# Layer 1 of a four-layer state-space network: 64x64 sums, and four of sixteen state inputs made by TensorE; in layer 3 the norm at another place

## The chip, the cores and the metric

One core of a Trainium2 chip runs the whole network in one program. The metric is the device time of one execution in microseconds. The core's engines work side by side, each through its own in-order queue: TensorE (PE, matmuls), VectorE (DVE), ScalarE (ACT), GpSimd (POOL), and SyncE (SP), which issues most DMAs.

## The reference

The input is 8 images of 64 channels and 64x64 pixels, float32. Four layers follow each other; layers 1 and 3 matter here. Both hold a selective scan with 128 (layer 1) or 256 (layer 3) channels and 16 states. Cut to the scan of layer 1:

```python
dts, Bs, Cs = jnp.split(x_dbl, [DT_RANK, DT_RANK + N], axis=2)
delta = jax.nn.softplus(dts + dt_b[None, :, :, None])
...
def step(h, inp):
    u, d, b, c = inp
    dA = jnp.exp(d[..., None] * A)
    h = dA * h + d[..., None] * b[:, :, None, :] * u[..., None]
    y = jnp.sum(h * c[:, :, None, :], axis=-1)
    return (h, y)
```

Layer 1 does it in four directions: the pixels by rows, by columns, and both backwards; the four outputs are added, then come a norm over channels, a gate, a projection, a second norm and a feed-forward block with a 3x3 convolution. Layer 3 first scales each pixel by the root of the mean square over its channels (the "norm" of the title), and scans forwards and backwards along one image axis, then along the other.

## The kernel before, in words

`stream` (L462) runs the scans of layers 1, 2 and 3. A **step** is one block of 1024 columns with all 16 **states** n; the loop at L596 runs over states, i counts them through all steps. In layer 1 a step is image b, direction k (in the order `ways` = 1, 3, 2, 0; the odd ones go by columns) and quarter j: 8 x 4 x 4 = 128 steps. In layer 3 it is pass s, chunk c (half an image), group g and direction k: 2 x 16 x 4 x 2 = 256 steps, 8 to a chunk.

For each state of layer 1:

- SP loads row n of B and of C from HBM, broadcast to 128 partitions (`load`, L1339), B five states ahead, C three. B has 4 buffers, C 5.
- GpSimd makes du*B (`multiply_b`, L526), two states ahead, into one of 3 `hb` buffers.
- ScalarE makes dA = exp(dt*A) (`decay`, L520) into one of two PSUM tiles, so it waits for what read the tile two states before. After each scan it copies the last column to `carry` (L1350).
- VectorE scans (L550). It works on one state after the other, and the C product (L564) follows: by VectorE into `hc`, or, for the states in `shared` (1, 4, 7, 10, 13), by GpSimd in place on `h`, one state later.
- TensorE adds the product to `acc` in PSUM (`gather`, `add_up`, L310): a matmul with the identity, 128x128, for each half of the 1024 columns. It is issued two states after the scan. After state 15 `drain` (L1367, L1365) adds `acc` to the image y.

`prepare` (L1317) makes dt, du, B and C for the next step; in layer 1 it starts at state 2 (`start`) and takes a piece per state. The rest of layer 1 (the norms, the convolutions, the feed-forward block: `begin`, `finish`, `feed`) is written as tasks, cut by `yield` into pieces; `advance` (L437) puts a piece into the queues per state. A piece that yields True holds the one "mm" tile of PSUM (`pp`), and nothing else may start that needs it. [...]

Layer 3 uses the same loop with a written plan (`plan`, L2095) of where pieces of `prepare` go. Six states (`fed`: 1, 2, 5, 6, 9, 10) are `direct`: du*B doesn't come from GpSimd. du is turned by TensorE (L2196) into `duT`, B is put on the diagonal of 128x128 blocks in HBM (`place`, L2122) and loaded from there, and `expand` (L2202) multiplies both: 8 matmuls. For the states in `lent` (1, 5, 9) the result goes into a dA tile, and dA of these states goes to SBUF; for 2, 6, 10 it goes into the mm tile. The sums of layer 3 use 64x64 blocks (`quads`, L315), four matmuls that work in the four quarters of the array.

The norm of layer 3 is a task, `begin` (L2034), one per chunk: 8 loads of x; twice a Square (L2053), a mean by TensorE (L2056) and a copy (L2058); Sqrt (L2063), reciprocal (L2066), a trip through HBM to broadcast it, and four products on GpSimd (L2083). It is queued in `behind` by `done` (L2230), after the first step of the chunk before. Pieces that take the mm tile may run at states 7 and 11 only (`rooms`), at 7 only if no `finish` is in `urgent`; a held tile is given back at state 13 (`lets`), or at once where an expansion needs it (L538). While `urgent` holds a task, `behind` stands still.

Of the kernel before, what the change touches and what calls it, by code (L numbers as in the profile page):

```python
# [272 lines left out]
class Net:  # L273
# [163 lines left out]
    def advance(self, behind, room=True, calm=True):  # L437


        while True:  # L440
            queue = self.held or (self.urgent if self.urgent else behind)
            if not queue or not (room or queue[0].said is False):
                return
            task = queue[0]
            if task.calm and not calm:
                return
            task.step()
            self.held = queue if task.said is True else None
            if not task.over:
                return  # L450
            queue.popleft()
# [10 lines left out]
    def stream(self, pools, ahead, steps, behind, rest=None):  # L462
# [39 lines left out]
        def fetch(i):  # L502
            if i < total and not isinstance(bp, tuple):
                s = steps[i // NS]
                t = bp.tile(s.bc_shape, F32, name="bc")
                s.load(i % NS, t)
                B[i], CC[i] = t[:, 0, :] if direct(i) else s.spread(t, 0), s.spread(t, 1)
            elif i < total:
                B[i] = bp[0].tile([128, T], F32, name="b")
                steps[i // NS].load(i % NS, 0, B[i])  # L510
# [22 lines left out]

        def expand(i):
            if i < total and direct(i) and lent(i):
                hb[i] = steps[i // NS].expand(B.pop(i), pe.tile([128, T], F32, name="dA"))
            elif i < total and direct(i):
                while self.held:  # L538
                    self.release()
                hb[i] = steps[i // NS].expand(B.pop(i))  # L540
# [35 lines left out]
            steps[at].add_up(acc[at], hc.pop(i), n == 0 and not begun[at], n == NS - 1)  # L576

        begun = {}
        work, self.held, self.urgent = None, None, deque()
        Task(steps[0].prepare()).run()  # L580
        for i in range(ahead[0]):
# [14 lines left out]
        for i in range(total + 2):  # L596
# [20 lines left out]
            if plan:  # L617
                before, behind_scan = plan.get(n, (0, 0))
                for _ in range(before if work else 0):
                    work.step()  # L620
                work = None if work and work.over else work
                if 2 < i <= total + 2 and shared(i - 3):
                    gather(i - 3)
                if 1 < i and not first and not shared(i - 2):
                    gather(i - 2)
                self.advance(behind, n in steps[0].rooms and not (n == 7 and self.urgent))
                if n in steps[0].lets and self.held:
                    self.release()
                if i < total:
                    scan(i)  # L630
                work = begin_next()
                for _ in range(behind_scan if work else 0):
                    work.step()
                if first:
                    gather(i - 2)
                if i < total and not shared(i):
                    multiply_c(i)
                if not direct(i + 2):
                    decay(i + 2)
                elif lent(i + 2):  # L640
                    expand(i + 2)
                if direct(i + 3):
                    decay(i + 3)
                    if not lent(i + 3):
                        expand(i + 3)
                continue
# [16 lines left out]
            if i < total:  # L663
                if not shared(i):
                    multiply_c(i)
            decay(i + 2)
        steps[-1].drain(acc.pop(len(steps) - 1))
        steps[-1].done()
        while self.held:
# [289 lines left out]
    def layer1(self, src, dst):  # L959
        nc, tc, d = self.nc, self.tc, self.d  # L960
        mid = self.hbm["x1a"]
        with ExitStack() as ctx:
            pool = lambda n, b, **k: ctx.enter_context(tc.tile_pool(name="l1" + n, bufs=b, **k))
            cp, p1, p2, img, tp = pool("c", 1), pool("p1", 1), pool("p2", 2), pool("img", 2), pool("t", 5)
            pp = pool("pp", 1, space=PSUM)
            bp = pool("b", 4), pool("cc", 5)
            pools = (bp, pool("hb", 3), pool("hc", 3), pool("h", 3), two(pool), pool("pa", 1, space=PSUM))

            pp, tp = Choice(pp, pools[4], "dA"), Choice(tp, pools[3], "h")
# [169 lines left out]
            def finish(b, chunks=range(4)):  # L1139
# [5 lines left out]

                def centred(c):
                    ps = pp.tile([128, T], F32, name="mm")
                    self.mm(ps, cent1, y[:, c * T : c * T + T])
                    yield True
                    return ps  # L1150

# [2 lines left out]
                def output(c):  # L1154
# [6 lines left out]
                    yield  # L1161
                    nc.gpsimd.tensor_tensor(inv, inv, z, ALU.mult)
                    ps = pp.tile([128, T], F32, name="mm")
                    self.mm(ps, cent1, y[:, at])
                    yield True
                    yield True
                    nc.vector.tensor_tensor(inv, ps, inv, ALU.mult)
# [21 lines left out]
            def feed(b, part=None):  # L1189
# [80 lines left out]
                for c in range(4):  # L1270
                    if c < 3:
                        yield from normed(c + 1)
                    yield from gated(c)

            def view(t, k, c):

                if k % 2 == 0:
                    return t[:, c * T : c * T + T].rearrange("p (a b) -> p a b", b=HW)
                return t.rearrange("p (a b) -> p b a", b=HW)[:, c * 16 : c * 16 + 16, :]
# [18 lines left out]
                            break  # L1298


            ways = (1, 3, 2, 0)

            class Step:
                start, early, late = 2, 8, True
                plan, direct, add_up = None, (), staticmethod(self.plain_sum)
                shared = (1, 4, 7, 10, 13)
                shaped = staticmethod(lambda t: t)

                def __init__(self, b, k, j):
# [7 lines left out]
                def prepare(self):  # L1317
                    k = self.k
                    u = self.u = view(images[self.b]["u"], k, self.c)
                    pd = pp.tile([128, T], F32, name="mm")[:68]  # L1320
                    net.mm(pd, xp[:, k, :], u)
                    yield True
                    dbl = p1.tile([68, T], F32, name="dbl")
                    nc.scalar.copy(dbl, pd)
                    self.bc = hp.tile([2 * NS, T], F32, name="bc")
                    nc.scalar.dma_start(self.bc, dbl[4 : 4 + 2 * NS])
                    pt = pp.tile([128, T], F32, name="mm")
                    for r in range(2):
                        at, o = slice(r * C, r * C + 4), slice(r * 512, r * 512 + 512)
                        nc.tensor.matmul(pt[:, o], dtw[at, k, :], dbl[at, o], start=True, stop=True)  # L1330
                    yield True
                    yield CALM
                    dt = self.dt = p2.tile([128, T], F32, name="dt")
                    net.softplus_act(dt, pt, dtb[:, k : k + 1])
                    yield False
                    du = self.du = p2.tile([128, T], F32, name="du")
                    nc.gpsimd.tensor_tensor(like(du, u), like(dt, u), u, ALU.mult)

                def load(self, n, m, t):  # L1339
                    nc.sync.dma_start(t, self.bc[m * NS + n : m * NS + n + 1, :].to_broadcast([128, T]))  # L1340
# [6 lines left out]
                def keep(self, n, h):  # L1347
# [3 lines left out]
                    if n == NS - 1:  # L1351
                        images[self.b]["carry"] = self.carry

                def skip(self, acc):
                    if self.k == 0:
                        net.mm(acc, skip[:, 0, :], self.u, start=True, stop=False)
                    return self.k == 0

                def drain(self, acc):
                    hold = images[self.b]  # L1360
                    if self.k == ways[0] and self.j == 0:
                        hold["y"] = img.tile([128, L], F32, name="img")
                    y = view(hold["y"], self.k, self.c)
                    if self.k == ways[0]:
                        nc.scalar.copy(y, like(acc, y))  # L1365
                    else:
                        nc.vector.tensor_tensor(y, like(acc, y), y, ALU.add)  # L1367

                def done(self):
                    b = self.b  # L1370
# [14 lines left out]
            with tc.manual_schedule():  # L1385
# [7 lines left out]
                    begun[1] = Task(begin(1))  # L1393
                    behind.append(begun[1])
                steps = [Step(b, k, j) for b in range(NB) for k in ways for j in range(4)]
                self.stream(pools, (5, 2, 3), steps, behind, rest)


    def layer2(self, src, dst):
# [516 lines left out]
    def layer3(self, src, dst):  # L1916
# [8 lines left out]
        with ExitStack() as ctx:  # L1925
# [108 lines left out]
            def begin(s, c):  # L2034
# [5 lines left out]
                from_ = srcs[s][q, rows, part * 4 * W : (part + 1) * 4 * W].rearrange("p (s t) -> p s t", t=HW)  # L2040
                for g in range(4):
                    at = slice(g * H, g * H + H)
                    for r in range(2):
                        nc.sync.dma_start(x[r * C : r * C + C, at, ends[r]], from_[:, at])
                        yield False
# [35 lines left out]
                for g in range(4):  # L2081
                    at = slice(g * H, g * H + H)
                    nc.gpsimd.tensor_tensor(hold["xn"][:, at], x[:, at], inv[:, at], ALU.mult)  # L2083

                    for _ in range(9 if g < 3 else 1):
                        yield False

            behind = deque()
            begun = {}
            images = {}  # L2090

            class Step:
                bc_shape, start = [128, 2, W], 13
                direct, lent, rooms, lets = fed, (1, 5, 9), (7, 11), (13,)
                plan = {  # L2095
                    2: (0, 1), 3: (2, 0), 4: (1, 0), 5: (1, 0), 6: (0, 1), 7: (1, 0), 8: (1, 0), 9: (1, 0), 10: (0, 1), 11: (1, 0), 13: (0, 1), 15: (1, 0)
                }
# [132 lines left out]
                def done(self):  # L2230
                    hold = chunks[self.s, self.c]
                    if self.k == 1:
                        net.urgent.append(Task(finish(self.s, self.c, self.g, [hold["y0"], hold["y1"]])))
                    more = self.s * 2 * NB + self.c + 1
                    if self.k == 0 and self.g == 0 and more < 4 * NB:
                        at = divmod(more, 2 * NB)
                        begun[at] = Task(begin(*at))
                        behind.append(begun[at])

            def finish(s, c, g, ys):  # L2240
                w, dst = weights[s], dsts[s]
# [28 lines left out]
            with tc.manual_schedule():  # L2270
# [7 lines left out]
                steps = [  # L2278
                    Step(s, c, g, k) for s in range(2) for c in range(2 * NB) for g in range(4) for k in range(2)
                ]  # L2280
                self.stream(pools, (6, 3, 6), steps, behind)


# [24 lines left out]
```

## Time and profile before

| what | us |
|---|---|
| median of 3 runs | 23705.83 (23693.11 to 23708.08) |
| the profiled execution | 23722.93 |
| its span | 23721.1 |
| busy: TensorE / VectorE / ScalarE / GpSimd | 20265.6 / 21369.5 / 14934.6 / 20578.3 |
| layer 1, about 960 to 8250 | 7290 |
| layer 3, from about 11330 to the end | 12391 |

A profile line names the source line, the engine, the operation, and out<-in by the program's tile names; then the count, busy time in us and mean ns of one; after the bar the engine's idle time just before such instructions, and what ended it. In a timeline the first number is the start in us, the second how long it took, and the bracket holds the idle time before it and its releaser. Each float32 matmul is recorded as two instructions. A busy TensorE is not TensorE at its peak, since ends of matmuls are modelled.

### The profile page before, as it was taken

The numbers are of one execution on the slowest core, as the hardware profiler recorded it, in microseconds if no ns is written. First come the engines' busy times: TensorE is split into PE (matmuls) and PEld (weight loads), VectorE is DVE, ScalarE is ACT, GpSimd is POOL, SyncE is SP. The second block draws the span as 40 slices with busy tenths as digits, with TensorE's granted clock in tenths as the row PEclk, the third lists the DMA queues.
The fourth block names the chain that finished last, engine by engine and source line by source line (L and its number), as shares of the span: only waits on it lengthen the run. The fifth ranks groups of instructions, "written<-read, shape, count | busy, mean of one in ns | idle before, by whom it ended". The sixth has DMA issues, their size and how long they took to land. (4 is left out here: it accounts for less than half of the span.)

```text
span 23721.1 us, 288888 instructions
## 1 busy us (share of the span) xinstructions
PE 20265.6 (85%) x99226; PEld 9428.8 (40%) x99226; DVE 21369.5 (90%) x12265; ACT 14934.6 (63%) x19503; POOL 20578.3 (87%) x9876
## 2 busy tenths in 40 slices
PE   7778888888888888879888888888888888888888
PEld 5323333333333323322444444444444444444444
DVE  5599999999999859977899999999999999999999
ACT  5445555555555446632677777777777777777776
POOL 0499999999999849986899999999999999999998
PEclk9889999999999999999899999999999999999999
DMA  3599889898898849961566666666666666666665
GB/s 80 190 325 322 309 313 320 312 318 317 310 317 312 287 148 340 342 212 35 171 184 185 179 183 184 182 183 182 184 183 184 183 185 183 184 181 184 182 182 172
DMA packets 2857344, 5295.40 MB, mean 223 GB/s; under 512 B 1357208, under 2 KB 1363452, under 8 KB 2853568
## 3 DMA queue, kind: packets, MB, share of 16 engines
q1 hardware_dynamic: 2831296, 5213.58, 68.9%
q10 hardware_dynamic: 24576, 63.33, 0.7%
q8 instruction: 785, 12.86, 0.2%
q14 instruction: 687, 5.63, 0.1%
HBM read 5112.98 MB, written 162.40 MB: 222 GB/s over the span
## 5 line engine op out<-in xcount | busy, mean ns | idle before, releaser
L526 POOL TENSOR_TENSOR hb<-du,bc 128x1024 f32<-128x1024 f32 x3072 | 7222.3, 2363 | 665.9 <-DVE h L550 301.5
L550 DVE TENSOR_TENSOR_SCAN dA<-dA,hb 128x1024 f32<-128x1024 f32 x2488 | 5675.5, 2281 | 189.4 <-POOL hb L526 105.7
L526 POOL TENSOR_TENSOR hb<-du,b 128x1024 f32<-128x1024 f32 x2048 | 4877.0, 2410 | 468.6 <-DVE dA L550 215.7
L564 POOL TENSOR_TENSOR h<-h,bc 128x1024 f32<-128x1024 f32 x2208 | 5175.8, 2359 | 106.1 <-DVE h L550 90.9
L520 ACT ACTIVATE dA<-dt,w_A 128x512 f32<-128x512 f32 x5120 | 3522.2, 689 | 1483.8 <-DVE hc L564 706.8
L520 ACT ACTIVATE dA<-dt,w_l_A 128x1024 f32<-128x1024 f32 x2560 | 2857.3, 1117 | 1006.1 <-DVE hc L564 765.3
L310 PE MATMUL acc<-hc,ident 128*128 128x512 f32 x7040 | 3387.3, 618 | 89.2 <-DVE img L1367 48.0
L550 DVE TENSOR_TENSOR_SCAN dA<-dA,carry,hb 128x1024 f32<-128x1024 f32 x1320 | 3093.1, 2343 | 120.9 <-POOL hb L526 59.0
L564 DVE TENSOR_TENSOR hc<-dA,bc 128x1024 f32<-128x1024 f32 x2400 | 2937.8, 1224 | 141.4 <-issue 2.7
L310 PE MATMUL acc<-h,ident 128*128 128x512 f32 x3200 | 1865.3, 712 | 880.4 <-POOL h L564 855.3
L320 PE MATMUL acc<-h,ident 64*64 64x512 f32 x16384 | 2156.7, 626 | 459.5 <-POOL h L564 458.7
L2207 PE MATMUL dA<-bc,duT 128*128 128x128 f32 x12288 | 1862.7, 314 | 546.6 <-ACT z L2183 518.3
L310 PEld LDWEIGHTS acc<-hc,ident 128*128 128x128 f32 x7040 | 1397.0, 202 | 2091.4 <-issue 1726.8
L2207 PEld LDWEIGHTS dA<-bc,duT 128*128 128x128 f32 x12288 | 1704.1, 222 | 1176.8 <-ACT z L2183 696.4
L320 PE MATMUL acc<-hc,ident 64*64 64x512 f32 x16384 | 2108.2, 608 | 0.0
L520 ACT ACTIVATE hb<-dt,w_A 128x512 f32<-128x512 f32 x3072 | 2038.7, 711 | 9.9
L550 DVE TENSOR_TENSOR_SCAN h<-hb,mm 128x1024 f32<-128x1024 f32 x768 | 1741.6, 2268 | 219.6 <-PE acc L320 179.0
L550 DVE TENSOR_TENSOR_SCAN h<-hb,dA 128x1024 f32<-128x1024 f32 x768 | 1752.0, 2281 | 189.4 <-PE dA L2207 157.3
L564 DVE TENSOR_TENSOR hc<-dA,c 128x1024 f32<-128x1024 f32 x1408 | 1722.7, 1224 | 118.1 <-DMA c<-bc 5.7
L550 DVE TENSOR_TENSOR_SCAN h<-dA,hb 128x1024 f32<-128x1024 f32 x712 | 1622.7, 2279 | 27.3 <-ACT dA L520 26.4
L2207 PE MATMUL mm<-bc,duT 128*128 128x128 f32 x12288 | 1603.8, 287 | 1.4 <-ACT u L2141 1.4
L2207 PEld LDWEIGHTS mm<-bc,duT 128*128 128x128 f32 x12288 | 1556.8, 205 | 3.3 <-ACT u L2141 2.2
(336 smaller groups left out, 26794.5 us busy)
## 6 DMA issues: line engine op xcount, KB each, us to landing
bc<-bc SPq DMA_DIRECT2D x2560, 512.0 KB
b<-bc SPq DMA_DIRECT2D x2048, 512.0 KB
c<-bc SPq DMA_DIRECT2D x2048, 512.0 KB
bc<-bc SPq DMA_DIRECT2D x512, 1024.0 KB
bc<-dg SPq DMA_DIRECT2D x1536, 256.0 KB
bc<-bc SPq DMA_DIRECT2D x1536, 256.0 KB
tmp<-rs SPq DMA_DIRECT2D x93, 512.0 KB
raw<-x SPq DMA_DIRECT2D x256, 128.0 KB
```

The lines of the kernel that those rows point to most:

```text
L310: self.nc.tensor.matmul(o, lhsT, r, start=start, stop=stop)
L320: self.nc.tensor.matmul(acc[j * C : j * C + C, r * 512 : r * 512 + 512], lhsT(j)[at, at], rhs[at, j * 512 : j * 512 + 512], start=start, s ...
L520: nc.scalar.activation(o[:, cut], s.dt[:, cut], AF.Exp, scale=A[:, n : n + 1])
L526: nc.gpsimd.tensor_tensor(s.shaped(hb[i]), s.shaped(s.du), B.pop(i), ALU.mult)
L550: nc.vector.tensor_tensor_scan(h[:, way], dA[i][:, way], b[:, way], s.first(n), ALU.mult, ALU.add)
L564: engine.tensor_tensor(s.shaped(o), s.shaped(h), CC.pop(i), ALU.mult)
L2207: nc.tensor.matmul(hb[:, at], self.duT[:, at], diag[:, m * 128 : m * 128 + 128], start=True, stop=True)
```

## The change

In layer 1, states 1, 5, 9 and 13 become `direct` and `lent`: their du*B is made by TensorE from du turned by a matmul with the identity and from diagonal blocks of B. ScalarE makes the blocks in SBUF, 8 per state, as identity times a column of B turned (`bt`); two blocks follow each scan. GpSimd's C products grow from five states to seven. The sums of layer 1 go to four 64x64 matmuls, which changes the layout of y; `drain` and the mean taken of y (`centre_y`, six matmuls of 64 rows in place of two of 128) follow. `prepare` starts at state 0 instead of 2, and its new end waits for the last expansion of the step before, as `duT` has one buffer. C is loaded two states ahead with 4 buffers. In layer 3, each chunk's norm is queued one step earlier, its pieces may run at state 11 only or, where they need no mm tile, also past a waiting `urgent` task, and its last products follow each other every 6 states instead of 9.

```diff
@@ advance
-            queue = self.held or (self.urgent if self.urgent else behind)
+            queue = self.held or self.urgent or behind
+            if not self.held and self.urgent and behind and not room and self.urgent[0].said is not False and behind[0].said is False:
+                queue = behind
@@ stream: fetch, expand, and the end of the loop
+            elif i < total and direct(i):
+                B[i] = bp[0].tile([128, T], F32, name="b")
+                small.extend((i, piece) for piece in steps[i // NS].blocks(i % NS, B[i]))
...
             if i < total and direct(i) and lent(i):
+                while small and small[0][0] <= i:
+                    small.popleft()[1]()
+                if not plan:
+                    need(i, "duT")
...
-                self.advance(behind, n in steps[0].rooms and not (n == 7 and self.urgent))
+                self.advance(behind, n in steps[0].rooms)
...
+            for _ in range(2):
+                if small:
+                    small.popleft()[1]()
             decay(i + 2)
+            expand(i + 2)
@@ layer1
-            bp = pool("b", 4), pool("cc", 5)
+            bp = pool("b", 4), pool("cc", 4)
...
+            def quarters(acc, lhsT, rhs, k, start, stop):
+                for r in range(2):
+                    at = slice(r * C, r * C + C)
+                    for j in range(2):
+                        if k % 2 == 0:
+                            part = rhs[at, j * 8 : j * 8 + 8, :] if len(rhs.shape) == 3 else rhs[at, j * 512 : j * 512 + 512]
...
+                        else:
+                            part = rhs[at].rearrange("p (b o h a) -> p b o h a", b=16, o=4, h=2)[:, :, :, j, :]
...
+                        nc.tensor.matmul(o, lhsT[at, at], part, start=start, stop=stop)
...
-                start, early, late = 2, 8, True
-                plan, direct, add_up = None, (), staticmethod(self.plain_sum)
-                shared = (1, 4, 7, 10, 13)
+                start, early, late = 0, 8, True
+                plan, direct, lent = None, (1, 5, 9, 13), (1, 5, 9, 13)
+                shared = (1, 2, 5, 6, 9, 10, 13)
...
+                    for m in range(8):
+                        nc.tensor.matmul(
+                            pb[:, m * 4 : m * 4 + 4], dbl[:, m * 128 : m * 128 + 128], net.ident[:68, 5:18:4], start=True, stop=True
+                        )
+                    yield True
+                    self.bt = p2.tile([128, 32], F32, name="bt")
+                    nc.scalar.copy(self.bt, pb[:, :32])
...
+                    while spent[0] < len(self.direct) * (self.b * 16 + ways.index(self.k) * 4 + self.j):
+                        yield False
+                    yield
+                    px = pp.tile([128, T], F32, name="mm")
+                    for m in range(8):
+                        at = slice(m * 128, m * 128 + 128)
+                        nc.tensor.matmul(px[:, at], du[:, at], net.ident, start=True, stop=True)
+                    yield True
+                    duT = p1.tile([128, T], F32, name="duT")
+                    nc.scalar.copy(duT, px)
...
+                def blocks(self, n, t):
...
+                        return lambda: nc.scalar.activation(t[:, at], net.ident, AF.Identity, scale=self.bt[:, f : f + 1])
...
+                def expand(self, diag, hb):
...
+                        nc.tensor.matmul(hb[:, at], self.duT[:, at], diag[:, at], start=True, stop=True)
...
-                self.stream(pools, (5, 2, 3), steps, behind, rest)
+                self.stream(pools, (5, 2, 2), steps, behind, rest)
@@ layer3
+                    while g == 3 and net.urgent:
+                        yield False
...
-                    for _ in range(9 if g < 3 else 1):
+                    for _ in range(6 if g < 3 else 1):
...
-                direct, lent, rooms, lets = fed, (1, 5, 9), (7, 11), (13,)
+                direct, lent, rooms, lets = fed, (1, 5, 9), (11,), (13,)
...
-                    more = self.s * 2 * NB + self.c + 1
-                    if self.k == 0 and self.g == 0 and more < 4 * NB:
+                    more = self.s * 2 * NB + self.c + 2
+                    if self.k == 1 and self.g == 3 and more < 4 * NB:
```

## The prediction

> **What bounds the kernel now.** I read the chain first: it reaches back only a few us, so it says nothing of the stages. So I cut the span where the line numbers change (layer 1 from 960 to 8250 us, layer 3 from 11330) and asked for busy times by stage:
>
> ```profile
> core 0: us, PE busy (x) PEld busy (x) DVE busy (x) ACT busy (x) POOL busy (x), PEclk, DMA share, GB/s
> 960.00:8250.00 7290.00, 6172.72 (x13884) 2329.44 (x13883) 6664.02 (x3719) 3915.61 (x4877) 6779.89 (x2960) 0.93 0.90 315
> 11330.00:23721.00 12391.00, 10778.34 (x70081) 5695.81 (x70079) 11837.08 (x6429) 9140.43 (x12357) 11479.64 (x4985) 0.94 0.63 182
> ```
>
> The columns are busy us and, in brackets, instructions of each engine; the last three are TensorE's granted clock, DMA share and GB/s. Layer 1 has 128 steps: 57.0 us each, of which VectorE works 52.1, GpSimd 53.0, TensorE 48.2, ScalarE 30.6. Two engines are level at the top, and nothing is full. Layer 3 has 256 steps of 48.4 us, VectorE 46.2, GpSimd 44.8. Next VectorE's waits in layer 1 (us in total, times, longest):
>
> ```profile
> DVE dA L550 <- POOL hb L526: 113.1, 73, 47.7
> DVE dA L550 <- ACT dA L520: 102.2, 74, 3.0
> DVE tmp L1233 <- PE mm L1025: 71.4, 28, 6.2
> DVE tmp L1244 <- ACT tmp L1241: 69.4, 13, 5.4
> DVE h L550 <- ACT dA L520: 53.7, 30, 4.0
> DVE tmp L1167 <- POOL tmp L1162: 38.8, 25, 2.9
> ```
>
> No scan waits for a DMA. From VectorE's timeline I took the start of every sixteenth scan: steps with no image task (norm, convolution, feed-forward) beside them take 51.1 to 52.2 us, steps with one 54 to 61. The timeline gives the prices too:
>
> ```profile
> 4001.31 2.35 DVE L550 TENSOR_TENSOR_SCAN dA<-dA,carry,hb 128x1024 f32<-128x1024 f32 x1
> 4003.75 1.22 DVE L564 TENSOR_TENSOR hc<-dA,c 128x1024 f32<-128x1024 f32 x1
> 4004.89 2.34 DVE L550 TENSOR_TENSOR_SCAN h<-dA,carry,hb 128x1024 f32<-128x1024 f32 x1
> 4007.15 1.20 DVE L1111 TENSOR_TENSOR tmp<-mm,tmp 128x1024 f32<-128x1024 f32 x1
> ```
>
> From start to start, a state whose C product is VectorE's costs 3.58 us, one whose C product is GpSimd's ("shared") 2.26. So a quiet step is 11 x 3.58 + 5 x 2.26 + 1.25 for the drain = 51.9: VectorE never waits there. GpSimd's is 21 x 2.37 + 2.62 for du = 52.4. Both limit.
>
> **Layer 1, engine by engine, per step.** VectorE: two more shared states take two products away, 2 x 1.32 = 2.64 us; a quiet step becomes 49.3. If nothing new waits: 128 x 2.64 = 338 us. GpSimd: four B products go (4 x 2.41), two C products come (2 x 2.37): -4.9, 53.0 to 48.1. DMA: four of 32 broadcasts of 512 KB go; C is asked for two states ahead instead of three, but in the order that follows the tightest C (state 14, whose buffer comes free with GpSimd's product of state 10) still has some 5 us, and now only 5.7 us of scans' products wait for C in the whole layer: nothing.
>
> TensorE: the sums now take 11 x 1.94 + 5 x 2.32 = 32.9 (2735.2 us for 1408 sums, 1486.6 for 640). The 64x64 form is in layer 3:
>
> ```profile
> L320 PE MATMUL acc<-h,ident 64*64 64x512 f32 x16384 | 2156.7, 626 | 459.5 <-POOL h L564 458.7
> L2207 PE MATMUL dA<-bc,duT 128*128 128x128 f32 x12288 | 1862.7, 314 | 546.6 <-ACT z L2183 518.3
> L520 ACT ACTIVATE hb<-dt,w_A 128x512 f32<-128x512 f32 x3072 | 2038.7, 711 | 9.9
> ```
>
> 2156.7 us for 2048 sums is 1.05 each: 16.8. Added are four expansions (16 records each; 2.05 where nothing holds them), 2.06 for turning du and, with no near row, 1.3 to 2.1 for turning B. Sum: 48.2 - 32.9 + 16.8 + 8.2 + 2.1 + 1.5 = 43.8. In the odd directions the sums read runs of eight floats. Bounds: no penalty, or that of the read of u at L310, whose median is 1018 ns against 592 where it is contiguous (single floats, 256 B apart). Eight floats a run is far nearer the first; I take 1.05 x. One rule speaks against mixing forms: the Trainium skill, "TensorEngine Tiling (Array Packing)", Key Properties, says that changing the tiling mode drains TensorE. It gives no figure; at 0.11 us (what a 128x512 record lasts beyond its pitch) some 18 changes a step would add 2 us. Layer 3 mixes both forms, and at 12649 us a 64x64 sum starts 0.07 us before the modelled end of an expansion: I take zero; with the rule TensorE would be at 45.8, still under 49.3.
>
> ScalarE: 32 diagonal blocks of 128x128. No such row; the 512-wide one above takes 711 ns, the slope (1117-689)/512 = 0.84 ns a column: 390 ns, and neighbours overlap by 0.09, so 0.30 each. Below: a 128x64 ACTIVATE took 256 ns; above: L826, 64x256 with strided ends, 723. The row of like form decides. L1033 and L2265 run Identity without a table load, so none is added. 9.6 + 1.0 (duT) + 0.2 = 10.8: 30.6 to 41.4. It is hidden, but two blocks now stand between the carry copy and the next exponential. Tightest place: a shared state, then another scan: 0.03 + 0.10 (carry) + 0.60 + 1.11 + 0.05 = 1.89 within the 2.26 of that scan. It holds; without that cover each step would pay at seven places.
>
> New wait: an expansion is behind the sum of the state four earlier on TensorE, which waits for GpSimd's product. From the end of scan 1 GpSimd must do B4, C1, C2, B6, du, B7, B8, C5: 7 x 2.37 + 2.62 = 19.2, then sum 1.05, expansion 2.05, handovers 0.3: 22.6. VectorE comes to scan 9 after 22.35. So it is late by 0.25, again a little for scan 13: 0.4 a step, 50 us. GpSimd thus has slack only in the last four states.
>
> Steps with image tasks: the waits on GpSimd (113 + 39, less one of 47.7 at the layer's start, so 104) shrink by only a fifth, for that reason: -20. The 161 waits ended by ScalarE (274 us in all, carry and rs included) grow by the 0.60 of two blocks: +95. In feed-forward steps TensorE is full (57.0 busy of 61 from 3463 to 3524): four an image, seven images, 4.4 less work, 1.8 beyond what VectorE gives: -50. Layer 1: -338 + 50 - 20 + 95 - 50 = -263.
>
> **Layer 3.** Adding VectorE's idle entries by place: step 3 of each chunk idles 111.5 us over 30 chunks, ordinary steps 21 to 29. This is it:
>
> ```profile
> 12655.91 2.48 PE L310 MATMUL mm<-sq,mean 64*1 64x512 f32 x4 [1.72 <-ACT z L2183]
> 12658.31 3.78 PE L2207 MATMUL dA<-bc,duT 128*128 128x128 f32 x16
> 12658.62 1.00 ACT L2058 COPY sq<-mm 1x1024 f32<-1x1024 f32 x1
> 12661.88 2.90 PE L2207 MATMUL mm<-bc,duT 128*128 128x128 f32 x16
> 12662.20 2.29 DVE L550 TENSOR_TENSOR_SCAN h<-hb,dA 128x1024 f32<-128x1024 f32 x1 [2.24 <-PE dA L2207]
> ```
>
> The mean of the squares at n = 7 takes the one "mm" bank that state 10's expansion needs. In the changed order this mean sits at n = 11 of step 1, as the second sits at n = 11 of step 3 today, where nothing idles. Gain 2.75 x 31 = 85 us. What moves with it is hidden or unchanged: 8 loads of x, 2 of rs, a write and 8 of inv on SP (no scan of layer 3 waits for a DMA), two Squares (1.07) and two copies on ScalarE; the Sqrt with its table loads and the reciprocal (16 us of waits) stay in step 4. GpSimd's four products of 1.4 go from one plus a burst of three to every sixth state; the idle time at their places, 39 us after step 5 and 21 after step 7, moves rather than goes: 0, between -40 and +30.
>
> **Sum.** -263 - 85 = -348. The profiled execution took 23722.9 (span 23721.1), the median 23705.8, 17 less; against the median 23358.
>
> **Rivals.** (a) The above, 0.55, own range 23250 to 23440. (b) The odd directions gain nothing, because runs of eight floats cost TensorE the full 1.72 (sums 1.81, step 56) or because ScalarE's 41 us hold tasks and exponentials up: half of 338 goes, 23527; 0.21. For it: TensorE is at 85% now; against: it falls to 77%. (c) Half of the waits on GpSimd and TensorE (104 + 108) vanish, ScalarE's don't grow and expansions cost nothing: layer 1 -338 - 106 = -444, layer 3 -110: 23152; 0.12. (d) Slower: in the odd directions the four 64x64 streams take turns and are strided too: 1.94 x 1.72 = 3.34 a sum, TensorE 80 us a step against 57: +23.4 x 64 = 1500, less 150 and 85, so 1265 on top: 24970; 0.08. It turns the sign where a sum costs more than about 2.1 us; layer 3's 1.05 speaks against it. (e) No effect, because a new wait eats each product saved: 0.04.
>
> Range: 23080 to 23570, which leaves out the far end of (b), (d) and what lies below (c). About 0.2% (47 us) is what a measurement here tells from no change: faster 0.88, same 0.04, slower 0.08.
>
> **What would show it.** VectorE's hc at 1152 in layer 1 instead of 1408; quiet steps at 49.3 to 50; the sum near 1.05 in both kinds of direction; blocks at 0.30 to 0.39; GpSimd's B at 1536; step 3 of a layer-3 chunk idle like the others. I'd be wrong if waits for expansions pass 1 us a step, blocks cost over 0.48 each, or odd steps stay near 57.

## The result, and the profile after

The changed kernel takes 24340.29 us (median of 4 runs, 24320.71 to 24361.47) against 23702.19 before: 1.027 of it, with a 95% interval of 1.0252 to 1.0288. It is slower; the forecast was 348 us faster. The profiled execution took 24361.47 us, its span is 24359.7.

Layer 1 first, from its first scan to its last: 7273 us before, 7925 after. Layer 3, from its first drain to its last, went from 12324.0 to 12300.1. So the loss of 638 us is layer 1's, and layer 3 gave 24 instead of 85. Layer 1 by engine (the columns are those of the table in the prediction):

```profile
960.00:8880.00 7920.00, 6577.67 (x34850) 2972.30 (x34850) 6357.24 (x3448) 5150.84 (x9210) 6164.48 (x2695) 0.86 0.77 256
```

VectorE and GpSimd work less than before, as intended. TensorE, which was to go from 48.2 us a step to 43.8, went up to 51.4. VectorE's idle time in this layer rose from 553 us to 1532, the wait before the layer's first scan included. Its waits after (us in total, times, longest):

```profile
DVE h L559 <- PE dA L1417: 834.6, 308, 12.6
DVE dA L559 <- ACT dA L525: 238.9, 151, 55.3
DVE h L559 <- ACT dA L525: 62.9, 31, 8.4
DVE tmp L1258 <- ACT tmp L1255: 62.6, 6, 10.7
DVE rs L1076 <- ACT rs L1074: 59.3, 14, 9.3
```

The first row is new: 308 of 512 scans of direct states wait for their expansion. The waits on GpSimd that led the list before are gone from its top. Now the groups that the prediction costed (count, busy us and mean ns of one record):

```profile
L1417 PE MATMUL dA<-b,duT 128*128 128x128 f32 x8161 | 1341.3, 331 | 321.7 <-ACT duT L1401 154.4 <-ACT carry L1431 119.3 <-DVE hc L573 41.5
L1302 PE MATMUL acc<-hc,ident 64*64 64x512 f32 x9168 | 1335.4, 663 | 19.7 <-ACT img L1456 12.3 <-DVE hc L573 6.7 <-DVE img L1458 0.5
L1302 PE MATMUL acc<-h,ident 64*64 64x512 f32 x7136 | 1126.5, 695 | 448.3 <-POOL h L573 448.3
L1374 PE MATMUL mm<-ident,dbl 68*128 68x4 f32 x2048 | 265.7, 262 | 38.9 <-ACT dbl L1369 30.5
L1409 ACT ACTIVATE b<-ident,bt 128x128 f32<-128x128 f32 x4086 | 1410.6, 394 | 240.6 <-POOL hb L531 208.8 <-ACT dbl L1369 12.3 <-DMA b<-bc 4.5
```

The sums of GpSimd's products (third row) are the ones to look at: TensorE stands still for 448 us ahead of them, waiting for GpSimd. Everything behind them in its queue waits as long.

An undisturbed step shows what this does. Below are entries of TensorE, VectorE and GpSimd from one such step:

```profile
1602.46 2.38 POOL L531 TENSOR_TENSOR hb<-du,b 128x1024 f32<-128x1024 f32 x1 [1.13 <-DVE h L559]
1604.81 4.65 POOL L573 TENSOR_TENSOR h<-h,c 128x1024 f32<-128x1024 f32 x2
...
1607.19 1.99 PE L1302 MATMUL acc<-h,ident 64*64 64x512 f32 x8 [4.53 <-POOL h L573]
1609.11 3.78 PE L1417 MATMUL dA<-b,duT 128*128 128x128 f32 x16
...
1613.00 2.35 DVE L559 TENSOR_TENSOR_SCAN h<-hb,carry,dA 128x1024 f32<-128x1024 f32 x1 [1.29 <-PE dA L1417]
...
1620.18 1.98 PE L1302 MATMUL acc<-h,ident 64*64 64x512 f32 x8 [2.20 <-POOL h L573]
```

GpSimd starts the B product of a state late, because its buffer is held by a scan (1.13 us); two C products follow as a pair; TensorE idles 4.53 us for the first of them; then the sum takes 1.99 us instead of 1.05 and the expansion 3.78 instead of 2.05, and the scan waits 1.29 us. Over nine undisturbed steps (1395 to 1875 us) the expansion is waited for 28.0 us, 3.1 a step. The doubled durations go with the granted clock, the third number from the end in these rows:

```profile
1599.66:1606.48 6.82, 3.00 (x26) 0.89 (x25) 6.45 (x3) 4.63 (x10) 5.69 (x3) 1.00 0.90 273
1606.48:1613.31 6.83, 6.12 (x28) 4.10 (x32) 5.42 (x5) 3.35 (x8) 6.83 (x4) 0.50 0.80 255
1620.14:1626.96 6.82, 6.26 (x28) 4.10 (x32) 6.08 (x5) 3.79 (x8) 4.57 (x2) 0.50 0.83 276
```

Over layer 1 it is 0.86 in the mean, before 0.93. The Trainium skill, "TensorE: Matmul & The Clock Gate", section "HAM oscillation — how this bites in real kernels", says that idle gaps beyond about 3.4 us bring half rate. The gap of 4.53 us fits; the sum at 1620.18, at half clock after a gap of 2.20 us, does not. In layer 1 of this trace, 257 of the 360 changes to half clock had no gap of 3.4 us in the 6.8 us before them, so a gap of that length is not needed for it here.

A step with a feed-forward task, at its state 5, shows a second form:

```profile
3721.82 1.12 ACT L435 ACTIVATE dt<-mm,w_l_dtb 128x1024 f32<-128x1024 f32 x1
...
3724.09 3.85 PE L1031 MATMUL mm<-strip,hidden 128*128 128x512 f32 x6
3727.88 1.09 PE L1302 MATMUL acc<-h,ident 64*64 64x512 f32 x8
3728.89 2.05 PE L1417 MATMUL dA<-b,duT 128*128 128x128 f32 x16
...
3731.05 2.35 DVE L559 TENSOR_TENSOR_SCAN h<-hb,carry,dA 128x1024 f32<-128x1024 f32 x1 [5.11 <-PE dA L1417]
```

The task's convolution needs the one mm tile, which `prepare` holds until the softplus has read it (to about 3722.9); TensorE comes to it at 3724.09, after a sum. Its 3.85 us and the next sum then stand ahead of the expansion, and VectorE waits 5.11 us. State 5 alone has 470 of the 835 us, state 1 has 198, 13 has 105, 9 has 61.

### The profile page after: what moved, and what is told of

It is laid out like the page before. It is cut to its first block, busy times and chain, and to the rows that moved or that the text cites. A ratio compares the mean times of both kernels' runs of the same rounds, so it can differ in the third digit from the quotient of the medians.

```text
span 24359.7 us, 333301 instructions
## 1 busy us (share of the span) xinstructions
PE 20578.8 (84%) x120346; PEld 10017.6 (41%) x120346; DVE 21094.5 (87%) x12009; ACT 16186.4 (66%) x23855; POOL 19981.8 (82%) x9620
## 5 line engine op out<-in xcount | busy, mean ns | idle before, releaser
L559 DVE TENSOR_TENSOR_SCAN dA<-dA,hb 128x1024 f32<-128x1024 f32 x2424 | 5529.0, 2281 | 204.2 <-ACT dA L525 117.4
L573 POOL TENSOR_TENSOR h<-h,bc 128x1024 f32<-128x1024 f32 x2208 | 5179.7, 2360 | 118.5 <-DVE h L559 111.5
L531 POOL TENSOR_TENSOR hb<-du,b 128x1024 f32<-128x1024 f32 x1536 | 3666.4, 2397 | 1485.6 <-DVE h L559 965.2
L559 DVE TENSOR_TENSOR_SCAN dA<-dA,carry,hb 128x1024 f32<-128x1024 f32 x1128 | 2645.9, 2346 | 163.9 <-ACT dA L525 126.1
L320 PE MATMUL acc<-h,ident 64*64 64x512 f32 x16384 | 2164.4, 628 | 423.5 <-POOL h L573 422.7
L525 ACT ACTIVATE dA<-dt,w_l_A 128x1024 f32<-128x1024 f32 x2048 | 2265.7, 1106 | 382.9 <-DVE h L559 202.9
L559 DVE TENSOR_TENSOR_SCAN h<-hb,dA 128x1024 f32<-128x1024 f32 x896 | 2045.0, 2282 | 353.2 <-PE dA L1417 190.3
L573 POOL TENSOR_TENSOR h<-h,c 128x1024 f32<-128x1024 f32 x896 | 2098.4, 2360 | 160.7 <-ACT carry L1431 138.5
L1417 PE MATMUL dA<-b,duT 128*128 128x128 f32 x8192 | 1346.7, 332 | 323.1 <-ACT duT L1401 154.4
L1417 PEld LDWEIGHTS dA<-b,duT 128*128 128x128 f32 x8192 | 1239.1, 239 | 858.6 <-ACT carry L1431 282.0
L1409 ACT ACTIVATE b<-ident,bt 128x128 f32<-128x128 f32 x4096 | 1414.0, 394 | 243.0 <-POOL hb L531 210.5
L1302 PE MATMUL acc<-h,ident 64*64 64x512 f32 x7168 | 1131.8, 696 | 454.2 <-POOL h L573 454.2
```

The source lines that it names most:

```text
L320: self.nc.tensor.matmul(acc[j * C : j * C + C, r * 512 : r * 512 + 512], lhsT(j)[at, at], rhs[at, j * 512 : j * 512 + 512], start=start, s ...
L525: nc.scalar.activation(o[:, cut], s.dt[:, cut], AF.Exp, scale=A[:, n : n + 1])
L531: nc.gpsimd.tensor_tensor(s.shaped(hb[i]), s.shaped(s.du), B.pop(i), ALU.mult)
L559: nc.vector.tensor_tensor_scan(h[:, way], dA[i][:, way], b[:, way], s.first(n), ALU.mult, ALU.add)
L573: engine.tensor_tensor(s.shaped(o), s.shaped(h), CC.pop(i), ALU.mult)
L1302: nc.tensor.matmul(o, lhsT[at, at], part, start=start, stop=stop)
```

## The experiments

All times are medians; ratios are to the kernel before, run on the same chip. The median of the kernel before differs by up to 30 us from one set of these runs to another (23699.68 to 23729.07), so a difference to the changed kernel is taken by way of the kernel before, which it exceeds by 638 us. The intervals of the ratios are about 35 us to either side.

### The sums alone

Edit, to the kernel before: `quarters`, `centre_y` and the drain of the changed kernel; no direct states, no layer 3.

```
-                plan, direct, add_up = None, (), staticmethod(self.plain_sum)
+                plan, direct = None, ()
...
+                def add_up(self, acc, hc, start, stop):
+                    quarters(acc, net.ident, hc, self.k, start, stop)
```

> The kernel before, with only the 64x64 sums of layer 1 (and the layout of y that goes with them). Theory Q (queue: in the changed kernel the expansions stand behind image-task matmuls, and behind what those wait for, in TensorE's in-order queue): nothing is expanded in layer 1 here, so the relief shows alone: 23600 to 23700 us, 0 to 100 below the kernel before. Theory C (clock: the shorter sums leave TensorE idle, so its granted clock falls from 0.93 to about 0.86 in layer 1, and what is left runs at half speed): clock in layer 1 down to 0.86 here too, and a time of 23750 or more.

Measured: 23585.86 us, 0.9955 (0.9942 to 0.9969), 114 us faster. Its layer-1 scans span 7123 us:

```profile
960.00:8080.00 7120.00, 5043.86 (x22626) 1370.18 (x22624) 6632.35 (x3707) 3912.39 (x4871) 6720.35 (x2954) 0.82 0.92 323
```

TensorE's busy time falls by 1129 us against the 6172.72 of before, the granted clock falls further than in the changed kernel (0.82), and it is faster all the same. A low clock alone is not the cause. A sum of eight records takes 1.09 us in the median in both kinds of direction; a step by columns fell from 57.4 to 55.9 us in the mean, one by rows from 56.4 to 55.5.

### The direct states with the plain sums

Edit, to the changed kernel: the sums, the centring and the drain of layer 1 go back to the form before.

```
-                def add_up(self, acc, hc, start, stop):
-                    quarters(acc, net.ident, hc, self.k, start, stop)
+                add_up = staticmethod(self.plain_sum)
```

> The changed kernel, with the 128x128 sums of before in layer 1. Theory C: TensorE has more to do, its clock in layer 1 stays at 0.92 or more, expansions take 2.05 us again, and most of the loss is gone: 23500 to 23800 us. Theory Q: the queue ahead of each expansion only gets longer (16 sums of 2 us in place of 1.05): 24350 to 25000 us, whatever the clock.

Measured: 24436.17 us, 1.0314 (1.0299 to 1.033). The clock is 0.95 in layer 1, the expansions take 2.06 us in the mean (2.63 in the changed kernel), and the scans still wait for them:

```profile
DVE h L559 <- PE dA L1417: 880.5, 294, 11.8
```

So the loss comes with the direct states and does not need the low clock. TensorE has more work here than in the changed kernel, though, so what the clock adds to the loss is not measured apart.

### Layer 3 alone

Edit, to the kernel before: the part of the diff that belongs to `advance` and layer 3 (among it `rooms` from (7, 11) to (11,)).

> The kernel before, with only the change in layer 3. The prediction gave it 85 us: 23617. Between the first and the last drain of layer 3 the changed kernel's trace is only 24 us shorter than before, with 59 us more of waits for ScalarE's exponentials of direct states; if that is due to the moved Square, this run gives about 23680. If it is 23617, the rest was lost to layer 1's change.

Measured: 23654.17 us, 0.9981 (0.9974 to 0.9987): 46 us. The idle time just before scans, added up over the 32 chunks by the step that the scan belongs to (0 to 7), fell in step 3 from 99 to 29 us, in step 4 from 67 to 33 and in step 0 from 79 to 65. It rose in step 1 from 27 to 37, in step 2 from 35 to 79 and in step 6 from 67 to 79. Two of its waits in layer 3, before and then in this run:

```profile
DVE h L550 <- PE dA L2207: 155.8, 188, 2.7
DVE h L550 <- ACT hb L520: 19.2, 13, 2.8
...
DVE h L552 <- PE dA L2216: 81.0, 189, 1.9
DVE h L552 <- ACT hb L522: 79.9, 54, 3.2
```

And one place in step 6:

```profile
13510.91 1.28 ACT L2150 ACT_TABLE_LOAD   x1
13514.63 1.27 ACT L2150 ACTIVATE u<-mm,w_cb 128x512 f32<-128x512 f32 x2 [2.44 <-PE mm L2139]
...
13517.21 1.33 ACT L522 ACTIVATE hb<-dt,w_A 128x512 f32<-128x512 f32 x2
```

The wait for the expansion fell from 155.8 to 81.0 us, the one for ScalarE's exponentials of direct states rose from 19.2 to 79.9. Most of the 79.9 us lie at state 1 of step 6 and state 2 of step 2 (46 and 29 us). In the second fence ScalarE has loaded the table of the convolution's activation and then stands 2.44 us in its queue for `prepare`'s convolution; the exponential behind it is late. That this convolution is late because of the moved mean was not tested.

### The task's piece behind the expansion

Edit, to the changed kernel: in states 3, 7, 11 and 15 the task's piece is issued after the expansion.

```
+            feeds = i + 2 < total and direct(i + 2)
+            if not feeds:
+                self.advance(behind, room, calm(i))
...
             expand(i + 2)
+            if feeds:
+                self.advance(behind, room, calm(i))
```

> The changed kernel; in the states of layer 1 that issue an expansion (3, 7, 11, 15) the image task's piece is put into the queues after the expansion instead of before it. No work is added or taken away. Theory Q: scan 5 waits 470 us for its expansion in the layer, scans 1, 9 and 13 another 365; half to two thirds of that goes: 23750 to 23950 us. Theory C: the clock stays at 0.86 and expansions stay slow, so no more than 100 us: 24240 to 24340. Theory A (ScalarE: its 16 us a step for blocks and turning hold the exponentials up): no change either, 24340.

Measured: 24469.66 us, 1.0323 (1.0308 to 1.0337). VectorE's waits in layer 1:

```profile
DVE dA L559 <- ACT dA L525: 347.6, 160, 56.6
DVE h L559 <- PE dA L1421: 324.7, 246, 6.0
DVE h L559 <- ACT dA L525: 256.3, 75, 12.1
DVE tmp L1262 <- ACT tmp L1259: 171.2, 17, 16.0
```

The wait that was aimed at fell from 834.6 to 324.7 (state 5 from 470 to 81). All of it came back, and more: ahead of the scans of states 0 and 2 (125 and 112 us to 342 and 239), in the tasks' own instructions on VectorE and in exponentials. Idle time of the layer is 1647 us against 1532.

### Without the two turns

Edit, to the changed kernel: no matmuls, tiles and copies for turning B and du; a constant column and du itself stand in.

```
-                    pb = pp.tile([128, T], F32, name="mm")
...
+                    self.bt = fixed
...
-                    px = pp.tile([128, T], F32, name="mm")
...
+                    self.duT = du
```

> The changed kernel with both turns left out: the eight small matmuls that turn B (a constant column stands in for it) and the eight that turn du (du itself is the left operand), with their copies. The expansions, the diagonal blocks, the shared states and the order of all else stay. What is left out of the computation: B and the turn of du at the four direct states. Theory 1 (the two turns make prepare take the one mm tile four times a step instead of two, so image tasks and expansions queue up behind each other on TensorE): waits of the scan for the expansion fall from 835 us in layer 1 to under 250, the scans of layer 1 from 7925 to about 7200, the time to 23550 to 23700. Rival 2 (an expansion placed in TensorE's in-order queue behind a task's matmuls is late whatever prepare does): they stay above 600, and the time falls by no more than the matmuls left out, to 24200 or so. Rival 3 (ScalarE's blocks): the same as rival 2 here.

### Without the blocks

Edit, to the changed kernel: one fixed tile of diagonal blocks for all direct states, and three buffers of B instead of four.

```
-                small.extend((i, piece) for piece in steps[i // NS].blocks(i % NS, B[i]))
+                B[i] = steps[i // NS].blocks(0, 0)
```

> The changed kernel with the 32 diagonal blocks a step left out: one fixed tile of diagonal blocks stands in (so B is left out at the direct states); both turns, the expansions and the order of all else stay; the B buffers go from four to three because the direct states need none. Theory 1 (the one mm tile): ScalarE has 10 us a step less, but the tile is taken as often; waits for the expansion stay above 600 us, and the time above 24150. Rival 3 (the blocks stand in ScalarE's queue ahead of the copies, softplus and exponentials that free the mm tile and start the scans): waits for the expansion fall below 400, those for the exponentials of direct states from 239 to under 80, and the time to 23900 or lower.

Measured, both on one chip: 24147.77 us without the turns, 1.0179 (1.0166 to 1.0193), and 24160.25 without the blocks, 1.0187 (1.0173 to 1.0201). That is 435 and 447 us above the kernel before, so 203 and 191 less than the changed kernel. The waits for the expansion, without the turns and then without the blocks:

```profile
DVE h L559 <- PE dA L1403: 632.3, 289, 8.8
...
DVE h L558 <- PE dA L1413: 803.7, 317, 12.3
```

Those at state 5 are 399 and 463 us. So the turns (by their hold on the one mm tile or by their 4 us a step on TensorE, which this run doesn't tell apart) and ScalarE's blocks each carry a part, and neither the larger one: both theories fall as the main cause. Taking either away left undisturbed steps at 52 to 54 us.

### The two parts that gain, together

Edit: the kernel before with the sums and the layer-3 part.

> The kernel before with both parts that gained alone: the 64x64 sums in layer 1 and the other place of the norm in layer 3; no direct states. If the parts don't touch each other: -114 and -46 against before, so about 23540 (23500 to 23580). If the layer-3 part gains less beside the other, as in the changed kernel's trace (-24): 23560.

Measured: 23570.94 us, 0.9936 (0.9922 to 0.995), 142 us faster than before. The parts nearly add up (114 + 46 = 160), and its median is the lowest of all, though its interval overlaps that of the sums alone. It also gives the price of the direct states with all that came with them in layer 1 (seven shared states, `prepare` from state 0, the order of C): 638 + 142 = 780 us. With the plain sums the price is as high: the run with plain sums less layer 3 alone, both on one chip, is 24436 - 23654 = 782 us.

### The sum behind the expansion, and both behind it

Edit, to the changed kernel: in the four states that issue an expansion, `gather(i - 2)` follows it; in the second run the task's piece too.

```
-            if late:
+            behind_expansion = late and i + 2 < total and direct(i + 2)
+            if late and not behind_expansion:
                 gather(i - 2)
...
             expand(i + 2)
+            if behind_expansion:
+                gather(i - 2)
```

> The changed kernel, complete, with one change of order: in the four states a step that issue an expansion (3, 7, 11, 15), the sum of the state two earlier, whose product GpSimd makes, is issued after the expansion instead of ahead of it. Theory A (the expansion stands on TensorE behind a sum that waits for GpSimd, and after that wait TensorE runs at half clock, so a sum of 2.0 us and an expansion of 3.8 follow it): undisturbed steps fall from 52.1 to 53.9 us to about 49.5 to 50.5, the waits for the expansion from 835 us by some 350 to 400 (3.1 a step are seen in undisturbed steps), and the time to about 23950. Rival B (the loss is in the image tasks' pieces and in prepare's turns, which stand ahead of the expansion too): undisturbed steps gain little, waits for the expansion stay above 650, time above 24200.

> As the run before, and the image task's piece of these four states is issued after the expansion too, as in the run that moved the piece alone, so that nothing that waits for another engine stands ahead of an expansion but the sum of the state before that. Theory A with the pieces: waits for the expansion below 150 us in layer 1, and little comes back elsewhere: idle time of VectorE in layer 1 from 1532 to some 700, the time 23450 to 23650. Rival C (the image tasks have too few states in which the mm tile is free, so their loss moves to states 0 to 2, as when the piece alone was moved, 24470): waits for the expansion fall as far, but idle time stays above 1100 and the time above 23900.

Measured: 24349.13 us, 1.0265 (1.0247 to 1.0282), and 24752.58, 1.0433 (1.0418 to 1.0449). In the first of them VectorE's wait for the expansion and TensorE's own waits show what takes the place of the wait for GpSimd:

```profile
DVE h L559 <- PE dA L1420: 656.0, 299, 17.1
...
PE dA L1420 <- ACT carry L1434: 528.8, 198, 6.9
PE dA L1420 <- ACT duT L1404: 212.9, 49, 7.9
PE dA L1420 <- DVE hc L573: 165.8, 55, 8.4
```

With the sum gone from ahead of it, the expansion waits for its PSUM tile: the state two earlier has been scanned in that tile, and VectorE's product and ScalarE's copy of the carry must have read it. From then to the scan there is one state of VectorE's work, 3.58 us, for the handover and an expansion of 2.05 to 3.8 us. The nine undisturbed steps fell from 53.1 to 52.2 us in the mean, not to 50, and the scans waited 656 us for the expansion. VectorE's idle time in the layer is 1522 us (1532), so theory A fails as the whole of it, and in the second run idle time is 1906.

### No task piece at state 3

Edit, to the changed kernel: `if n != 3:` ahead of `self.advance(behind, room, calm(i))`.

> The changed kernel, complete, but no piece of an image task is issued at state 3 of a step, where the softplus has just been asked for and the expansion of state 5 follows. Theory A: state 5's waits (470 us of 835) fall below 150 and most of this is gained, as only one of 16 places is lost to the tasks: time about 24050. Rival C (the tasks' pieces, now later, are forced out at state 0 or stand ahead of the next expansion): what state 5 gains turns up at states 0, 2 and 9, time 24250 to 24500.

Measured: 24311.24 us, 1.0246 (1.0229 to 1.0263), 582 us above the kernel before. That is 56 us less than the changed kernel, at the edge of what the intervals tell apart. VectorE's idle time at state 5 fell from 521 to 138 us; at states 0, 1, 2 and 9 it rose from 125, 206, 112 and 66 to 222, 249, 334 and 132. That is what rival C had forecast.

### No expansions, and nothing at all for the direct states

Edit, to the changed kernel and to the kernel without the turns (there without blocks too):

```
-                    for m in range(8):
-                        at = slice(m * 128, m * 128 + 128)
-                        nc.tensor.matmul(hb[:, at], self.duT[:, at], diag[:, at], start=True, stop=True)
-                    return hb
+                    return self.duT
```

> The changed kernel without the four expansions a step: the scans of the direct states take the turned du from SBUF as their input instead (so B is left out there, and the blocks are made but not read). Both turns, the blocks, the seven shared states and the order of all else stay; each direct state also leaves one PSUM tile free. Theory A (the loss is that an expansion stands in TensorE's queue behind sums and task pieces that wait, and has only one state's 3.5 us between the release of its PSUM tile and its scan): the waits for the expansion, 835 us, go and little takes their place: scans of layer 1 from 7925 to about 7150 to 7250, undisturbed steps to 49.3 to 50, time 23550 to 23700. Rival C (tasks have too few free states, so time moves): idle time of VectorE in layer 1 stays above 1000, time above 23950.

> The changed kernel with no work at all for du*B of the four direct states: no turns, no blocks, no expansions (the scans take du itself, so B is left out there). What is left of the change: seven shared states, the 64x64 sums, layer 3. If the prediction's first term was right (2 x 1.32 us of VectorE a step are saved when nothing new waits): undisturbed steps at 49.3 us, scans of layer 1 at about 7123 - 338 = 6785 to 6850, time 23200 to 23270. If the shared states themselves wait (on GpSimd's products in pairs, carry copies, the one PSUM tile for image tasks): undisturbed steps stay at 50 or more, scans of layer 1 above 6950, time above 23380.

Measured: 24316.6 us, 1.0248 (1.0233 to 1.0263), and 24167.14, 1.0187 (1.0172 to 1.0203). Taken at face value the second would say that even four free states cost 438 us. Its scans say otherwise. The direct states by form, in the run with nothing left of the direct work:

```profile
L558 DVE TENSOR_TENSOR_SCAN dA<-dA,carry,hb 128x1024 f32<-128x1024 f32 x864 | 2024.2, 2343 | 10.4 <-ACT carry L1413 7.2 <-ACT dA L524 2.2
L558 DVE TENSOR_TENSOR_SCAN h<-hb,carry,du 128x1024 f32<-128x1024 f32 x384 | 1719.3, 4477 | 8.5 <-ACT carry L1413 6.1 <-ACT hb L524 2.5
```

A scan that reads decay and input both from SBUF took 4477 ns in the mean and up to 7.8 us; with one of them in PSUM it takes 2343. The 128 such scans that start without a carry took 4315, against 2284. That is (4477 - 2344) x 384 + (4315 - 2284) x 128 = 1079 us that the experiment added itself. VectorE is idle 295 us in the whole layer there. Taking the 1079 us off its 7729 us of scans gives 6650, below the 6785 that the prediction's first term asks for; but this is a calculation, since slow scans also gave the other engines time. Both runs are inconclusive on the question they were made for. A version with the exponentials of these states in PSUM, which has no such pair of reads, was not run.

## Why the prediction was wrong

**What failed: the wait for the expansions.** The prediction put it at "0.4 a step, 50 us". It was 3.1 us in an undisturbed step and 835 us in the layer, 6.5 a step. Its terms for layer 1 beside the trace, in us (waits from the layer's first scan on):

| term | forecast | measured |
|---|---|---|
| VectorE's own work, with gaps up to 0.15 us | -338 | -320 |
| waits for the expansions | +50 | +835 |
| waits that GpSimd ends | -20 | -99 |
| waits that ScalarE ends | +95 | +186 |
| other waits that TensorE ends | -50 | +24 |
| the rest (waits for DMAs, and small) | 0 | +26 |
| sum | -263 | +652 |

The prediction's sum for the expansion walked GpSimd's queue as if GpSimd never waited. In the nine undisturbed steps GpSimd waited 53 us, 6 a step, for buffers that scans held: the exponentials of direct states now live in the same three hb buffers. It also took 1.05 and 2.05 us for what follows the wait, where at half clock it was 1.99 and 3.78. And it looked only at undisturbed steps: that tasks' pieces and `prepare`'s turns go down TensorE's queue ahead of an expansion was not in it. It had the right queue and named the point from which it would be wrong ("if waits for expansions pass 1 us a step").

**The quiet step.** 49.3 was forecast; nine such steps took 53.1 in the mean (52.0 to 54.5), more than the 51.9 of the same nine before. VectorE's two products are gone (1152 in the layer), but 35 us of waits in nine steps, 3.9 each, took their place: 49.3 and 3.9 make about the 53.1 measured.

**TensorE's relief.** 48.2 was to become 43.8 and came out at 51.4: the sums (1335.4 + 1126.5) at 19.2 us a step instead of 16.8 and the expansions at 10.5 instead of 8.2, as part of both ran at half clock, and the turn of B at 2.08, the upper end of its bounds. Most of the other 2.3 lies in matmuls that the prediction left as they were: the mean of y, six matmuls now (114.5 us to 239.1), the convolutions at L1031 (454.6 to 521.5) and dt (149.8 to 209.0). The -50 for feed-forward steps had no ground then.

**ScalarE.** The blocks were costed well: 0.69 us a pair against 0.60. But the waits that ScalarE ends rose by 186 us, twice the 95 forecast.

**Layer 3.** Its mechanism was right: the wait in step 3 went, 70 us of it. The forecast of 85 was a little high, since the 111.5 us that it starts from hold about 16 us of the reciprocal's wait for the Sqrt, which stayed. Step 4 gave 34 more. What the moved work would meet was put at nothing; steps 1, 2 and 6 lost 66 us, mostly to ScalarE's exponentials. 46 alone, 24 in the changed kernel.

**What was right.** The 64x64 sums show no penalty for runs of eight floats (1.09 us a sum in both kinds of direction), and rival (d), the only slower one, did not happen. The kernel became slower by another mechanism, nearest to rival (e), a new wait that eats what is saved. That had a chance of 0.04 and was taken as no worse than no change; but a new wait can be longer than what it eats.

**What is shown and what is not.** Shown: the direct states, with what came with them, cost 780 us over the other two parts, and 782 with the plain sums at a clock of 0.95, so the loss does not need the low clock; the turns and the blocks carry 203 and 191 us when taken away one at a time; four changes of order at the expansions each cut the wait they aimed at, and none gained more than 56 us. Not settled: the remaining 390 us or so (if the two add up, which was not tried). The waits moved from TensorE's queue to the PSUM tile, to ScalarE and to the tasks, which points to a ring of in-order queues without slack rather than to one place; that is argued from the four runs, not shown. Fewer direct states, a fourth hb buffer, fewer C products in pairs on GpSimd, or a later start of `prepare` were not tried.

## What to carry to other kernels

An operation that moves to an engine with free time joins a queue: ask what stands ahead of it there, what that waits for, and how long the buffer it writes has been free when it must be done. Here 2 us of TensorE work had 3.6 us between the release of its PSUM tile and its reader, and every piece of a task ahead of it was late work for the bottleneck. When a change has parts, the parts that only make an engine's work shorter (the 64x64 sums: 114 us) were safer here than the part that added a handover between three engines.

## What the hardware showed beyond this

- A scan with both inputs in SBUF took 4.48 us beside a busy GpSimd, 2.34 with one in PSUM. In the run without expansions, 14 of the 512 such scans had no GpSimd instruction beside them and took 2.31 in the mean. The Trainium skill, "SBUF — State Buffer", section "SBUF: two separate sides", has the rule: VectorE with two SBUF inputs and a GpSimd operation that reads SBUF lock each other out of a shared port for the whole instruction. The trace agrees: a GpSimd product takes 2.4 us, and the scan is longer by 2.1 in the mean.
- Lighter work can lower TensorE's clock: 0.93 before, 0.82 with the 64x64 sums alone, and that kernel was faster by 114 us.
